# Squares for the key and query norms: one ScalarE instruction per PSUM bank, summed on VectorE

## The chip, the cores and the metric

The kernel runs on one core of a Trainium2 chip. The metric is the device time of one execution in microseconds; a time given for a kernel is the median of its runs.

## The reference

A decoder layer of three blocks, each followed by a residual add and a LayerNorm, for 4 batches of 256 tokens of width 512. The first block is a small attention inside each token; the third is a top-8 mixture of 64 bias vectors. The second, where nearly all the work is, is a cross attention with 32 query heads in 8 groups of 4, over 1601 context rows and the 256 tokens themselves. Its queries and keys are normalized over their 128 numbers per head before the scores are formed:

```python
def rms_norm(x, w):
    var = jnp.mean(jnp.square(x.astype(jnp.float32)), axis=-1, keepdims=True)
    return (x.astype(jnp.float32) * jax.lax.rsqrt(var + EPS)).astype(x.dtype) * w

kv = jnp.concatenate([context, latents], axis=1)
q = (latents @ Wq).reshape(bsz, q_len, HEADS, HEAD_DIM).transpose(0, 2, 1, 3)
k = (kv @ Wk).reshape(bsz, kv_len, KV_HEADS, HEAD_DIM).transpose(0, 2, 1, 3)
v = (kv @ Wv).reshape(bsz, kv_len, KV_HEADS, HEAD_DIM).transpose(0, 2, 1, 3)
q = rms_norm(q, q_norm_w)
k = rms_norm(k, k_norm_w)
scores = jnp.einsum('bhgqd,bhkd->bhgqk', qg, k) * scale
probs = jax.nn.softmax(scores.astype(jnp.float32), axis=-1).astype(q.dtype)
out = jnp.einsum('bhgqk,bhkd->bhgqd', probs, v)
...
return out @ Wo
```

## The kernel before

**Units and heads.** The cross attention is cut into 32 units: 4 batches times 8 key/value heads, batch by batch. A unit has 4 query heads. Products are made as three fp16 matmuls of high and low parts (`mm3`, lines 241 to 243), so fp32 accuracy comes from fp16 operands.

**The work of a unit on keys and values.** The 1857 rows of a batch are 15 tiles of 128 rows (the last one of 65), taken as 7 pairs and one single. `kv_proj` projects a pair into one PSUM bank `kvp` (for each tile 128 columns of keys and 128 of values). ScalarE then squares the keys of each tile with `accum_out`, which gives the sum over the 128 columns in `kss` (L403). GpSimd scales the sums and takes them to the power of -1/2 (L405, L406: `krk`). ScalarE writes the high part of the values `Vh` (L411) and VectorE the low part `Vl` (L412). `kv_n` is emitted later: ScalarE writes the normalized keys' high part `kh` (L426), VectorE the low part (L428), which also releases the bank. A DMA transposes `kh` into `KT`.

**The work of a unit on queries.** `q_proj` projects each of the 2 tiles of 128 tokens into one bank `qp` (4 heads of 128 columns). ScalarE squares each head with `accum_out` into `qss` (L449), GpSimd makes `qrq` (L451, L452), VectorE the normalized queries `qn` (L459), and `q_tr` splits and transposes them. The tile `qn` has one buffer: it receives the squares first, and the normalized queries then overwrite them.

**The work of a head.** `qk` makes the scores of a pair of key tiles in a bank `s`; ScalarE copies it to SBUF (L498) and VectorE takes a running maximum (L502, L504, L507), after which the bank is free. `qmax`, `qmax_t` and `qmax_b` find and spread the maximum (L514 to L536). `soft` subtracts it on VectorE (L545), makes the exponentials on ScalarE (L553, L554) and the low part on GpSimd (L555); in batch 0 one of four chunks is done with one exponential and a GpSimd copy (L550, L551). `pv` multiplies with the values (L574 to L576), `oevac` divides (L584 to L593), `wout` applies the output weights.

**Order.** Every step is put on a list with a position, in units of heads, from tables of offsets (`AT`, `F0` for batch 0, `LAST` for the last 4 units), and the list is emitted in order of position; the start has an order written out by hand (`START`), in which two units and the first block's attention share the engines. The framework's scheduler then orders the instructions on each engine from its own timeline model (`schedule_with_timeline_sim=True`), so a change of one instruction can move others. Each engine runs its instructions in the order that results.

**PSUM.** Six banks with the tag `u` serve `kvp`, `qp`, `s`, the output products and transposes alike; one bank each serves the maxima and the sums of `pv`.

Of the kernel before, what the change touches and what calls it, by code (L numbers as in the profile page):

```python
# [12 lines left out]
AF = mybir.ActivationFunctionType  # L13
ALU = mybir.AluOpType
AX = mybir.AxisListType
# [3 lines left out]
P = 128  # L19
# [32 lines left out]
def tile_decoder(ctx: ExitStack, tc: tile.TileContext, x, cx, Wq1, bq1, Wk1, bk1, Wv1, bv1,  # L52
                 Wq, Wk, Wv, Wo, qnw, knw, rw, rb, eb, out):
    nc = tc.nc
# [7 lines left out]
    G = Wq.shape[1] // Wk.shape[1]  # L62
# [174 lines left out]
    def mm3(dst, quads, start=True, stop=True, skip=False):  # L237

        n = len(quads)
        for k, (ah, al, bh, bl) in enumerate(quads):  # L240
            nc.tensor.matmul(dst, ah, bh, start=start and k == 0, stop=False, skip_group_check=skip)  # L241
            nc.tensor.matmul(dst, ah, bl, start=False, stop=False, skip_group_check=skip)  # L242
            nc.tensor.matmul(dst, al, bh, start=False, stop=stop and k == n - 1, skip_group_check=skip)  # L243
# [64 lines left out]
    def nk(t):  # L308
        return REM if t == NT - 1 else P

    def kview(tile_, t):

        o = (t % 2) * 2 * NC * P
        return tile_[:, o:o + 2 * NC * P].rearrange("p (l c k) -> p l c k", l=2, c=NC)[:, :, :, :nk(t)]

    def tiles_of(p):
        return [t for t in (2 * p, 2 * p + 1) if t < NT]
# [57 lines left out]
    KT, VT, QT = {}, {}, {}  # L375
    kns, qns = {}, {}
    PW = XS * WS

    kring = [const.tile([P, NT, 2, P], F16, name=f"KT_{i}") for i in range(2)]
    VR = 19  # L380
# [9 lines left out]
    def kv_proj(u, p):  # L390
        h, b = units[u]
        wkv = Wt["kv", h]
        ts_ = tiles_of(p)
        n = len(ts_)
        k = nk(ts_[0])
        ps = psu.tile([P, 2, 2 * P], F32, tag="u", name=f"kvp_{u}_{p}")
        for j, t in enumerate(ts_):
            v = kview(kvt[u, p], t)
            mm3(ps[:k, j, :], [(v[:, 0, c], v[:, 1, c], wkv[:, 0, c], wkv[:, 1, c]) for c in range(NC)])
        ss = p2.tile([P, 2], F32, tag="kss", name=f"kss_{u}_{p}")  # L400
        kn = p2.tile([P, 2, P], F32, tag="kn", name=f"kn_{u}_{p}", bufs=2)
        for j in range(n):
            nc.scalar.activation(kn[:k, j, :], ps[:k, j, 0:P], AF.Square, accum_out=ss[:k, j:j + 1])  # L403
        rk = p2.tile([P, 2], F32, tag="krk", name=f"krk_{u}_{p}")
        nc.gpsimd.tensor_scalar(ss[:k, :n], ss[:k, :n], 1.0 / (P * QS * QS), 1e-6 * PW * PW / (QS * QS), ALU.mult, ALU.add)  # L405
        nc.gpsimd.tensor_tensor(rk[:k, :n], ss[:k, :n], mhalf[:k, :n], ALU.pow)  # L406
        v = NPAIR * u + sum(q[0] == u for q in vuse.values())
        assert v < VR or ("pv", *vuse[v - VR]) in done
        vuse[v] = (u, p)
        vh, vl = VT[u, p] = vring[v % VR]  # L410
        nc.scalar.activation(vh[:k, :n, 0:P], ps[:k, :n, P:], AF.Copy, scale=VS / PW)  # L411
        nc.vector.scalar_tensor_tensor(vl[:k, :n, :], ps[:k, :n, P:], VS / PW, vh[:k, :n, 0:P],  # L412
                                       ALU.mult, ALU.subtract)
        kns[u, p] = (kn, rk, ps)
# [25 lines left out]
    def q_proj(u, i):  # L440
        h, b = units[u]
        wq = Wt["q", h]
        ps = psu.tile([P, G, P], F32, tag="u", name=f"qp_{u}_{i}")
        v = kview(kvt[u, TL], NF + i)
        mm3(ps.rearrange("p g d -> p (g d)"), [(v[:, 0, c], v[:, 1, c], wq[:, 0, c], wq[:, 1, c]) for c in range(NC)])
        ss = p2.tile([P, G], F32, tag="qss", name=f"qss_{u}_{i}")
        qn = p2.tile([P, G, P], F32, tag="qn", name=f"qn_{u}_{i}", bufs=1)
        for g in range(G):
            nc.scalar.activation(qn[:, g, :], ps[:, g, :], AF.Square, accum_out=ss[:, g:g + 1])  # L449
        rq = p2.tile([P, G], F32, tag="qrq", name=f"qrq_{u}_{i}")  # L450
        nc.gpsimd.tensor_scalar(ss, ss, 1.0 / P, 1e-6 * PW * PW, ALU.mult, ALU.add)  # L451
        nc.gpsimd.tensor_tensor(rq, ss, mhalf[:, :G], ALU.pow)  # L452
        qns[u, i] = (qn, rq, ps)
# [237 lines left out]
    for i in range(NQ):  # L691
        first[f"a{i}"] = lambda i=i: next(x0[i], None)
        first[f"lwq{2 * i}"] = lambda i=i: wload_q(0, 2 * i)
        first[f"wq{2 * i}"] = lambda i=i: wprep_q(0, 2 * i)
        for k, f in (("qproj", q_proj), ("qnorm", q_n), ("qturn", q_tr)):
            first[f"{k}{i}"] = lambda f=f, i=i: f(0, i)
# [4 lines left out]
    for p in range(NPAIR):  # L701
        for k, f in (("load", src_load), ("make", kv_make), ("keep", lambda b, p: kv_keep(b, p, kvt[b, p]))):
            first[f"{k}{p}"] = lambda f=f, p=p: f(0, p)
        for k, f in (("proj", kv_proj), ("norm", kv_n), ("turn", kv_tr)):
            first[f"{k}{p}"] = lambda f=f, p=p: [f(u, p) for u in range(HB)]
# [54 lines left out]
    for u in range(U):  # L760
        h, b = units[u]
        A = par(u)
        if u > 0:
            t0 = 4 * (u - 1)
            if u > 1:
                at(t0 - 0.01, proj_new, u)
            steps = [("kv", p) for p in range(NPAIR) if p != TL]
            z = A["z0"] if h == 0 else A["z1"]
            steps[z:z] = [("kv", TL), ("q", 0), ("q", 1)]
            if u == 1:  # L770
                steps = [("q", 0), ("q", 1)] + 8 * [("", 0)]
            step = A["span"] / len(steps)
            for k, (what, v) in enumerate(steps):
                pos = t0 + step * k
                norm, turn = min(pos + A["norm"] * step, 4 * u - 0.006), min(pos + A["turn"] * step, 4 * u - 0.005)
                if what == "kv" and u > 1:
                    at(pos - A["lead"] * step, kv_load, u, v)
                    at(pos, kv_proj, u, v)
                    at(norm, kv_n, u, v)
                    at(turn, kv_tr, u, v)  # L780
                elif what == "q":
                    at(pos, q_proj, u, v)
                    at(norm, q_n, u, v)
                    at(turn, q_tr, u, v)
        z = "l" if u == U - 1 else ""
        for g in range(G):
            n = 4 * u + g
# [55 lines left out]
```

## Time and profile before

| | before |
|---|---|
| median of 3 runs | 2420.73 us (2419.91 to 2424.31) |
| profiled execution | 2421.83 us, span 2420.1 us |
| granted TensorE clock, mean | 0.991 |
| DMA | 338.82 MB, mean 140 GB/s |
| squares of keys with sums (L403), ScalarE | 480 squares, 480 read-outs of the sum |
| squares of queries with sums (L449), ScalarE | 256 squares, 256 read-outs of the sum |

The page lists busy time by engine, then by line: the line and engine, the operation, what it writes and reads, the count, the busy time, the mean of one in ns, and the idle time just before, with what ended it. Matmuls overlap in TensorE's pipeline, so the mean of one is longer than the time from one start to the next. ScalarE's and VectorE's rows overlap a little too.

### The profile page before, as it was taken

How to read it: one execution, taken by the hardware profiler on the slowest of the kernel's cores; microseconds unless marked ns; L12 is line 12 of the kernel's file. 1: busy time of each engine (PE TensorE's matmuls, PEld its weight loads, DVE VectorE, ACT ScalarE, POOL GpSimd, SP SyncE). 2: the span in 40 equal slices, each digit the busy share in tenths (PEclk: the TensorE clock that was granted, in tenths of full speed). 3: DMA queues.
4: the chain of work that ended last, by engine and by line, in shares of the span. 5: the costliest groups of instructions: out<-in, count | busy, mean ns of one | idle time of the engine just before them, and what ended most of it. 6: DMA issues, size and time to landing. Idle time of an engine off the chain costs nothing.

```text
span 2420.1 us, 65667 instructions
## 1 busy us (share of the span) xinstructions
PE 2347.3 (97%) x25424; PEld 2003.1 (83%) x25424; DVE 1909.9 (79%) x3747; ACT 2051.1 (85%) x4672; POOL 1538.5 (64%) x1367
## 2 busy tenths in 40 slices
PE   7799999999999999999999999999999999999997
PEld 5587888888888878888888888888888888888885
DVE  8788978987877788787777788787777778777775
ACT  4798898888888878889888888888889888889884
POOL 2377776776666655776656666666666655657554
PEclk9999999999999999999999999999999999999997
DMA  8946776666564546555545555455644543554310
GB/s 267 245 100 160 185 175 178 185 153 156 137 164 112 148 139 166 139 142 125 151 128 129 156 142 137 140 138 121 156 116 113 131 122 109 140 131 105 98 35 27
DMA packets 393345, 338.82 MB, mean 140 GB/s; under 512 B 318532, under 2 KB 328260, under 8 KB 384840
## 3 DMA queue, kind: packets, MB, share of 16 engines
q1 hardware_dynamic: 393032, 334.63, 53.0%
q8 instruction: 199, 3.26, 0.6%
q14 instruction: 114, 0.93, 0.2%
HBM read 219.98 MB, written 38.80 MB: 107 GB/s over the span
## 4 chain that ended last, share of the span: by engine, by line
PE 74%; ACT 8%; DVE 7%; issue 5%; POOL 4%; DMA 2%; SPq 0%; POOLq 0%; DVEq 0%; ACTq 0%
PE o L574 7%; PE o L576 7%; PE o L575 7%; PE kvp L241 7%; PE kvp L243 7%; PE s L241 7%; PE kvp L242 7%; PE s L243 7%; PE s L242 7%; PE wo L241 2%; PE wo L242 2%; PE wo L243 2%; POOL P L555 2%; DVE S L545 2%; ACT P L553 2%
## 5 line engine op out<-in xcount | busy, mean ns | idle before, releaser
L555 POOL TENSOR_TENSOR P<-S,P 128x1024 f16<-128x1024 f32 (+1 forms) x512 | 1032.3, 2027 | 435.3 <-ACT S L554 410.3
L574 PE MATMUL o<-Vh,P 128*128 128x129 f16 (+1 forms) x3840 | 696.1, 221 | 6.8 <-ACT P L553 2.9
L576 PE MATMUL o<-Vh,P 128*128 128x129 f16 (+1 forms) x3840 | 695.8, 220 | 3.6 <-POOL P L555 3.6
L575 PE MATMUL o<-Vl,P 128*128 128x128 f16 (+1 forms) x3840 | 695.0, 219 | 0.0
L498 ACT COPY S<-s 128x512 f32<-128x512 f32 (+1 forms) x1024 | 568.3, 594 | 81.8 <-PE s L243 75.4
L553 ACT ACTIVATE P<-S,lnps 128x1024 f16<-128x1024 f32 (+1 forms) x480 | 530.9, 1117 | 48.1 <-DVE S L545 46.8
L545 DVE TENSOR_TENSOR S<-S,mt 128x1024 f32<-128x1024 f32 (+1 forms) x512 | 557.8, 1146 | 13.1 <-PE mt L536 12.2
L554 ACT ACTIVATE S<-S,lnps 128x1024 f32<-128x1024 f32 (+1 forms) x480 | 538.4, 1126 | 0.2
L241 PE MATMUL s<-QT,KT 128*128 128x256 f16 x1920 | 524.0, 273 | 14.1 <-ACT S L498 3.1
L243 PE MATMUL s<-QT,KT 128*128 128x256 f16 x1920 | 523.9, 273 | 0.0
L242 PE MATMUL s<-QT,KT 128*128 128x256 f16 x1920 | 523.7, 273 | 0.0
L504 DVE TENSOR_TENSOR M<-s,M 128x512 f32<-128x512 f32 x640 | 438.5, 685 | 99.8 <-ACT S L498 79.6
L574 PEld LDWEIGHTS <-P 128*128 128x128 f16 (+1 forms) x3840 | 376.1, 98 | 24.6 <-DVE oh L593 3.3
L241 PE MATMUL kvp<-wkv_back,kv 128*128 128x256 f16 (+1 forms) x1440 | 392.6, 273 | 1.8 <-DVE rl L584 0.6
L243 PE MATMUL kvp<-wkv_back,kv 128*128 128x256 f16 (+1 forms) x1440 | 392.6, 273 | 0.0
L242 PE MATMUL kvp<-wkv_back,kv 128*128 128x256 f16 (+1 forms) x1440 | 392.6, 273 | 0.0
L575 PEld LDWEIGHTS <-P 128*128 128x128 f16 (+1 forms) x3840 | 377.4, 98 | 14.7
L576 PEld LDWEIGHTS <-P 128*128 128x128 f16 (+1 forms) x3840 | 375.6, 98 | 5.0 <-POOL P L555 3.8
L241 PEld LDWEIGHTS <-kv 128*128 128x128 f16 (+1 forms) x2040 | 201.5, 99 | 48.0 <-issue 8.0
L243 PEld LDWEIGHTS <-kv 128*128 128x128 f16 (+1 forms) x2040 | 201.4, 99 | 47.1
L242 PEld LDWEIGHTS <-kv 128*128 128x128 f16 (+1 forms) x2040 | 201.4, 99 | 41.4 <-issue 1.7
L241 PEld LDWEIGHTS <-KT 128*128 128x128 f16 x1920 | 188.0, 98 | 33.1 <-issue 5.5
(177 smaller groups left out, 4164.2 us busy)
## 6 DMA issues: line engine op xcount, KB each, us to landing
kv<-kvd SPq DMA_DIRECT2D x210, 512.0 KB, 3.7
wq_back<-wqd SPq DMA_DIRECT2D x24, 1024.0 KB, 6.2
wo_back<-wod SPq DMA_DIRECT2D x24, 1024.0 KB, 5.2
kvd<-kvm SPq DMA_DIRECT2D x28, 512.0 KB, 3.1
cst<-in_ctx_dram SPq DMA_DIRECT2D x24, 512.0 KB, 5.8
wkv_back<-wkvd SPq DMA_DIRECT2D x24, 512.0 KB, 4.2
st_q<-in_L_xattn_Wq_dram SPq DMA_DIRECT2D x17, 512.0 KB, 4.8
wqd<-wq SPq DMA_DIRECT2D x8, 1024.0 KB, 6.1
```

What stands on the lines that cost most here:

```text
L241: nc.tensor.matmul(dst, ah, bh, start=start and k == 0, stop=False, skip_group_check=skip)
L242: nc.tensor.matmul(dst, ah, bl, start=False, stop=False, skip_group_check=skip)
L243: nc.tensor.matmul(dst, al, bh, start=False, stop=stop and k == n - 1, skip_group_check=skip)
L498: nc.scalar.copy(sv, ps[:, :m, :])
L504: nc.vector.tensor_tensor(Mx[n], ps, Mx[n], ALU.max)
L545: nc.vector.tensor_tensor(sv, sv, Mb[n].unsqueeze(1).broadcast_to([P, m, S]), ALU.subtract)
L553: nc.scalar.activation(pt[:, 0, :m, :], sv, AF.Exp, bias=lnps, scale=ES)
L554: nc.scalar.activation(sv, sv, AF.Exp, bias=lnps, scale=ES)
L555: nc.gpsimd.tensor_tensor(pt[:, 1, :m, :], sv, pt[:, 0, :m, :], ALU.subtract)
L574: nc.tensor.matmul(a[:, :P + 1], ph, v1[:k], start=t == 0 and i == 0, stop=False, skip_group_check=True)
L575: nc.tensor.matmul(a[:, :P], ph, v0[:k], start=False, stop=False, skip_group_check=True)
L576: nc.tensor.matmul(a[:, :P + 1], pl, v1[:k], start=False, stop=t == NT - 1 and i == NQ - 1, skip_group_check=True)
```

## The change

The squares of a bank are made by one ScalarE instruction without a sum: two tiles of keys together (256 columns), and the four heads of a query tile together (512 columns). VectorE then adds them up over the innermost 128 columns. The switch `SQE` selects VectorE for the sum (1) or GpSimd; it is 1. GpSimd's steps, and everything behind them, stay as they are. The lines of the kernel below the first added line move down by one.

```diff
@@ -375,6 +375,7 @@
     PW = XS * WS
+    SQE = 1
@@ -399,8 +400,8 @@ def kv_proj
         ss = p2.tile([P, 2], F32, tag="kss", name=f"kss_{u}_{p}")
         kn = p2.tile([P, 2, P], F32, tag="kn", name=f"kn_{u}_{p}", bufs=2)
-        for j in range(n):
-            nc.scalar.activation(kn[:k, j, :], ps[:k, j, 0:P], AF.Square, accum_out=ss[:k, j:j + 1])
+        nc.scalar.activation(kn[:k, :n, :], ps[:k, :n, 0:P], AF.Square)
+        (nc.vector if SQE else nc.gpsimd).tensor_reduce(ss[:k, :n], kn[:k, :n, :], AX.X, ALU.add)
@@ -445,8 +446,8 @@ def q_proj
         ss = p2.tile([P, G], F32, tag="qss", name=f"qss_{u}_{i}")
         qn = p2.tile([P, G, P], F32, tag="qn", name=f"qn_{u}_{i}", bufs=1)
-        for g in range(G):
-            nc.scalar.activation(qn[:, g, :], ps[:, g, :], AF.Square, accum_out=ss[:, g:g + 1])
+        nc.scalar.activation(qn, ps, AF.Square)
+        (nc.vector if SQE else nc.gpsimd).tensor_reduce(ss, qn, AX.X, ALU.add)
```

## The prediction

> **What bounds the kernel now.** I read the page first. Its first part gives the busy time of each engine, and the stretch sums cut the span into start, batch 0, the long middle and the end (columns: span of the stretch, then busy time and count of PE, PEld, DVE, ACT, POOL, the granted clock, DMA share, GB/s).
>
> ```profile
> PE 2347.3 (97%) x25424; PEld 2003.1 (83%) x25424; DVE 1909.9 (79%) x3747; ACT 2051.1 (85%) x4672; POOL 1538.5 (64%) x1367
> ```
>
> ```profile
> 0.00:120.00 120.00, 86.58 (x667) 68.24 (x668) 95.70 (x175) 73.72 (x212) 38.50 (x82) 0.95 0.90 258
> 120.00:580.00 460.00, 451.29 (x4981) 389.09 (x4980) 387.48 (x721) 401.83 (x905) 338.66 (x283) 0.99 0.65 162
> 580.00:2340.00 1760.00, 1748.29 (x19170) 1498.72 (x19169) 1374.83 (x2745) 1529.70 (x3491) 1125.00 (x983) 1.00 0.50 132
> 2340.00:2420.00 80.00, 61.16 (x615) 47.02 (x612) 51.91 (x108) 45.88 (x66) 36.37 (x22) 0.84 0.07 23
> ```
>
> TensorE is the bound. It stands still for 72.8 us in all (2420.1 - 2347.3): 33.4 in the first 120 us, 8.7 up to 580, 11.7 in the next 1760, 18.8 at the end. The change takes no work from TensorE, so what it can win lies in these 72.8 us alone, and the 20.4 us between 120 and 2340 are the part that ScalarE and VectorE, as feeders, can touch. What it can lose has no such bound. Next, the waits of PE alone show whom the feeders make late.
>
> ```profile
> PE kvp L241 <- DVE M L504: 5.7, 6, 1.9
> PE s L241 <- ACT S L498: 3.1, 5, 0.9
> PE o L576 <- POOL P L555: 3.6, 1, 3.6
> ```
>
> VectorE is named more often than ScalarE. Summed over the rows of that view between 120 and 580 us, PE waits 7.7 us for VectorE and 0.8 for ScalarE; between 580 and 2340, 7.5 and 3.8. So the engine that gets work is the one that already holds TensorE up, and the engine that is relieved hardly does.
>
> **The change, ScalarE's side.** 32 units of work each make 7 full pairs of key tiles, one part pair of 65 rows and 2 query tiles. The timeline of ScalarE gives the pace (start of a row to start of the next).
>
> ```profile
> 1199.48 0.57 ACT L498 COPY S<-s 128x512 f32<-128x512 f32 x1
> 1199.95 1.15 ACT L553 ACTIVATE P<-S,lnps 128x1024 f16<-128x1024 f32 x1
> ...
> 1201.25 0.29 ACT L449 ACTIVATE qn<-qp 128x128 f32<-128x128 f32 x1
> ...
> 1202.26 1.18 ACT L554 ACTIVATE S<-S,lnps 128x1024 f32<-128x1024 f32 x1
> ...
> 1204.12 0.30 ACT L403 ACTIVATE kn<-kvp 128x128 f32<-128x128 f32 x1
> 1204.28 0.24 ACT L403 ACTIVATION_READ_ACCUMULATOR kn<-kvp 128x1 f32 x1
> ...
> 1204.62 0.43 ACT L411 ACTIVATE Vh<-kvp 128x256 f16<-128x256 f32 x1
> 1204.89 0.64 ACT L498 COPY S<-s 128x512 f32<-128x512 f32 x1
> ```
>
> Each square with a sum is two instructions, the second one reading out the sum. Four of them for a query tile hold ScalarE for 1.01 us (1201.25 to 1202.26), two for a key pair for 0.50 (1204.12 to 1204.62). One instruction on 256 columns of a bank paces at 0.27 (L411), on 512 at 0.47 (L498); one on 128 at 0.16, its read-out not counted. Saved: 224 x 0.23 = 51.5, 64 x 0.54 = 34.6, 32 x 0.09 = 2.9, together 89 us, 2.8 per unit of some 72 us. The Trainium skill, page "ScalarE: Activation LUTs", section "What ACT_TABLE_LOAD costs", prices an ACTIVATE with immediate operands at 186 ns + 0.833 ns per column, 93 ns of it overlapped, and has no price for the read-out. By it the saving would be an estimated 39 us (224 x 0.09 + 64 x 0.28), less than half; the relief below would shrink with it, and the total would come out 0.6 us higher.
>
> **VectorE's side.** It gets 320 reduces. For 128x256 the nearest row is L214, also a reduce of 256 numbers a row: 0.33 us on the chain. For 128x512 it is L514, with L504, an elementwise operation of the same size, as the control.
>
> ```profile
> L504 DVE TENSOR_TENSOR M<-s,M 128x512 f32<-128x512 f32 x640 | 438.5, 685 | 99.8 <-ACT S L498 79.6 <-DVE M L504 0.5
> L514 DVE TENSOR_REDUCE M<-M 128x256 bf16<-128x512 f32 x128 | 89.2, 697 | 3.8
> ```
>
> 697 ns alone, and 0.60 when packed (a 512-column step of L502 on the chain). 224 x 0.33 = 73.9, 64 x 0.60 = 38.4, 32 x 0.20 = 6.4 (between the 163 ns of a two-element reciprocal, L584, and 0.33): 119 us, 3.7 per unit; by full durations (697, and 418 as the 256-column Vl step L412 takes) some 143. A rule speaks against the move: the Trainium skill, "VectorE: DVE Perf Modes", section "Rules for kernel authors", calls `tensor_reduce` the slowest operation of the engine. The rows do not bear that out at this size, 697 against 685, so I charge no extra; a reduce twice as slow as elementwise work would make it about 240 us.
>
> What of this is covered? In the built order nearly every reduce stands just ahead of the Vl of its own pair (L412 before). The waits show VectorE idle there: DVE Vl L412 <- ACT Vh L411, 78.4 us in 82 waits, about 1 us each. The square now ends 0.5 us sooner than Vh did, so in those 82 of 256 the reduce (0.33) lies in idle time and costs nothing. For the others it pushes what is queued behind it: Vl, then the L504 maxima that free PSUM banks, and the subtractions L545 before the exponentials. POOL's two small steps (L405, L406) now wait for the reduce, and the L555 behind them too; but POOL has 36% idle, and PE waits for L555 once, 3.6 us, so I price this at nothing, with up to 1 us per unit if VectorE is late.
>
> **The start.** From 20 to 56 us the chain runs almost only on VectorE, because both units' pairs and the small attention share it.
>
> ```profile
> 31.10 0.33 DVE big L214
> ...
> 70.33 1.15 ACT qn L449 x8
> ```
>
> Eight reduces stand in VectorE's order before the row that ends this stretch: 8 x 0.33 = +2.6 us. ScalarE's saving there is not on that path. The query squares on the chain, 1.15 us, become 0.47 + about 0.6 + a hand-over: no change.
>
> **The sum.** From 120 to 580 us VectorE gets 6.4 units x 3.7 = 24 us; its free share falls from 15.8% to 10.5%. If PE's wait on it goes as the inverse, 7.7 becomes 11.6: +3.9. From 580 to 2340, 92 us: free share 21.9% to 16.7%, 7.5 becomes 9.8: +2.3. A third of it is covered as above: 6.2 x 0.68 = 4.2. ScalarE's free share rises by about 4 points everywhere; the 4.6 us waited on it fall by a quarter: -1.1. Sum: 2.6 + 4.2 - 1.1 = +5.7 us. The profiled execution took 2421.83 (span 2420.1), 1.1 above the median of 2420.73 and within the spread of the three runs, so the forecast is 2420.73 + 5.7 = 2426.4, say 2426.5. 0.2%, about what a measurement of this kernel can tell from no change, is 4.8 us.
>
> **Rivals.** *ScalarE's relief counts after all (faster).* Half of the 20.4 us of mid idle goes because S copies (L498) and exponentials come sooner, and the start's reduces fit the gaps marked "issue" on the chain: 10.2 less 2 lost on VectorE, 2412 to 2413. For it: ScalarE is the fuller feeder (85%), and VectorE waits 79.6 us on the copies of L498. Against it: PE itself hardly waits for ScalarE. It decides if VectorE's idle time covers over two thirds of the reduces rather than one.
> *All covered (no change).* VectorE has 510 us idle and takes 119; if the start's 2.6 are hidden too, only the scheduler's reshuffle is left, about 2421.
> *VectorE clogs batch 0 (clearly slower).* At 89% to 92% a burst of four L545 (1.13 us each) with a reduce ahead of it delays maxima and so PSUM banks: a further 1.5 us in each of 6.4 units, and half of that later, 24 x 0.3: about 2440. For it: VectorE's slices at 90% and PE's waits on L504 lie in this stage. It decides from about 93% of VectorE between 240 and 480 us.
> *It does not do what it says.* The built order has 320 squares instead of 736, and 320 reduces on VectorE, none on POOL, so I give this no chance.
>
> **How the numbers follow.** Mildly slower, as summed (2425.6 to 2433): 0.30. Clogged: 0.14. No change (2415.9 to 2425.6): 0.29. Faster: 0.27. The instructions are ordered anew on every engine: of the 320 small POOL steps, 75 stand before or behind another L555 than they did. That moves small idle times in either direction and keeps the other cases near. The range leaves about one in ten at each end: 2412 (the relief case) to 2443 (clogged, with 3 us more at the start).
>
> **What would show it.** Right: no read-out rows on L403/L449's successors, ScalarE down by 60 to 90 us, VectorE up by 110 to 145, PE idle in the first 120 us up from 33.4 to about 36, PE's waits on VectorE rows up by 3 to 5, on ScalarE rows down. Wrong: PE's mid idle falls below 15 us (relief wins), reduces well over 0.45 us, POOL's L555 among PE's waits, or a lower granted clock.

## The result, and the profile after

The changed kernel takes 2463.05 us, the median of 4 runs (2457.03 to 2465.57), against 2420.93 (2419.91 to 2424.31) before: a ratio of 1.0166, 95% interval 1.0154 to 1.0178, or 42 us more. The profiled execution took 2461.62 us, with a span of 2459.8 and a mean granted clock of 0.988 (0.991 before). Forecast were 2426.5 and a range up to 2443. The sign was right; the size was 6 us instead of 42.

Busy time by engine, from the page of the kernel after:

```profile
PE 2357.5 (96%) x25424; PEld 2006.5 (82%) x25424; DVE 2024.8 (82%) x4067; ACT 1972.8 (80%) x3520; POOL 1533.7 (62%) x1367
```

ScalarE lost 78 us and VectorE gained 115, as forecast (-89 and +119). TensorE stands still for 102.3 us (2459.8 - 2357.5) instead of 72.8. These 29.5 us and 10.2 us of longer busy time, at a granted clock that is 0.3% lower (0.3% of 2347 is 7 us), make up the span's 39.7.

The stretch sums of the kernel after (columns as before):

```profile
0.00:120.00 120.00, 88.56 (x646) 67.73 (x646) 94.39 (x184) 58.70 (x128) 31.07 (x78) 0.93 0.82 236
120.00:580.00 460.00, 428.56 (x4671) 365.80 (x4670) 399.64 (x746) 373.53 (x653) 324.79 (x268) 0.99 0.60 158
580.00:2340.00 1760.00, 1741.14 (x19076) 1494.13 (x19073) 1449.42 (x2972) 1462.34 (x2621) 1119.24 (x985) 1.00 0.50 133
2340.00:2460.00 120.00, 99.19 (x1041) 78.86 (x1038) 81.34 (x168) 78.24 (x122) 58.58 (x38) 0.90 0.11 31
```

Read the count behind TensorE's busy time as well as the time. In the first 120 us TensorE is busy for longer than before, at a lower clock, but has made 21 matmuls fewer; between 120 and 580 it makes 310 fewer and stands still for 31.4 us instead of 8.7. To follow this without the stretches' fixed edges, I matched the two traces by the last running maximum of each unit (L514 before, L515 after). The kernel after lags by 12.2 us at the end of unit 0, by 14.6 at unit 3, 21.3 at unit 4, 32.7 at unit 7, and by only 7 more at the end. So the start and batch 0 lose 33 us, and the other three batches 7.

From the waits of PE alone, kernel after, the rows on the maxima and the one on L556 (line waited for; us in all, times, longest):

```profile
PE kvp L241 <- DVE M L505: 7.7, 7, 1.5
PE wo L241 <- DVE M L505: 7.0, 2, 4.7
PE s L241 <- DVE M L505: 6.3, 12, 1.3
...
PE o L577 <- POOL P L556: 4.1, 2, 3.9
```

Before, the second of these rows was

```profile
PE wo L241 <- DVE M L504: 1.6, 1, 1.6
```

Most of it is a wait that was there before, only longer: a matmul wants a PSUM bank whose last reader is a maximum on VectorE (17.1 of the 26.2 us that PE waits for VectorE between 120 and 580 us). Summed as in the prediction, PE's waits on VectorE grow from 7.7 to 26.2 us between 120 and 580 us, and from 7.5 to 17.0 between 580 and 2340; its waits on ScalarE in the second of these stretches fall from 3.8 to 1.3, but in the first 120 us they grow from 2.7 to 7.3.

The reduce itself costs what was forecast (groups of VectorE by shape, kernel after: count, busy us, mean ns, then idle time before it and its releaser):

```profile
L404 DVE TENSOR_REDUCE kss<-kn 128x2 f32<-128x256 f32 x224 | 92.5, 413 | 55.1 <-ACT kn L403 54.6
L450 DVE TENSOR_REDUCE qss<-qn 128x4 f32<-128x512 f32 x64 | 43.7, 682 | 30.9 <-ACT qn L449 30.6
```

New is what stands behind it. GpSimd's own waits, first before, then after:

```profile
POOL kss L405 <- ACT Vh L411: 82.6, 21, 7.1
POOL kss L405 <- ACT kn L403: 63.6, 48, 14.7
POOL qss L451 <- ACT qn L449: 47.9, 33, 3.9
```

```profile
POOL kss L406 <- DVE kss L404: 233.5, 73, 17.3
POOL qss L452 <- DVE qss L450: 79.6, 33, 7.6
```

From 194 us to 313: GpSimd stands in its order in front of the two small steps of the norm and waits for the reduce, which has its own place in VectorE's queue. Matched row by row, the time from the end of the square to the finished norm grows from 3.20 to 5.05 us on average, and a bank `kvp` is held from its last matmul to its last read (L428, L429 after) for 10.68 instead of 9.22 us. The longest single stop of PE in batch 0 shows how such queues meet (timelines of GpSimd, VectorE, ScalarE and PE, kernel after):

```profile
447.46 7.89 POOL L556 TENSOR_TENSOR P<-S,P 128x1024 f16<-128x1024 f32 x4
450.07 5.58 DVE L215 TENSOR_TENSOR sc<-sc,mx 128x256 f32<-128x256 f32 x1
451.09 0.41 ACT L403 ACTIVATE kn<-kvp 128x256 f32<-128x256 f32 x1
455.56 0.68 DVE L505 TENSOR_TENSOR M<-s,M 128x512 f32<-128x512 f32 x1
456.30 0.61 PE L241 MATMUL wo<-wo,OT 128*128 128x512 f16 x1 [4.66 <-DVE M L505]
457.35 0.41 DVE L404 TENSOR_REDUCE kss<-kn 128x2 f32<-128x256 f32 x1
457.92 0.19 POOL L406 TENSOR_SCALAR kss<-kss 128x2 f32<-128x2 f32 x1 [2.20 <-DVE kss L404]
```

A small subtraction on VectorE (L215, median 0.43 us) lasts 5.58, until 0.3 us after GpSimd's four L556. The maximum behind it is late, and TensorE stands 4.66 us for its bank. The square made at 451.09 has its sum only at 457.76, and GpSimd has by then waited 2.20 us for it; before the change that sum would have been read out on ScalarE at once. What begins this stop, though, is the drawn-out subtraction (the last section shows why) and not the longer chain: the sum is late because of it. In the kernel before, three of the six such subtractions were drawn out too (1.05 to 1.95 us).

### The profile page after: what moved, and what is told of

Same layout as the page of the kernel before. It is cut to its first block, busy times and chain, and to the rows that moved or that the text cites. A ratio compares the mean times of both kernels' runs of the same rounds, so it can differ in the third digit from the quotient of the medians.

```text
span 2459.8 us, 64727 instructions
## 1 busy us (share of the span) xinstructions
PE 2357.5 (96%) x25424; PEld 2006.5 (82%) x25424; DVE 2024.8 (82%) x4067; ACT 1972.8 (80%) x3520; POOL 1533.7 (62%) x1367
## 5 line engine op out<-in xcount | busy, mean ns | idle before, releaser
L556 POOL TENSOR_TENSOR P<-S,P 128x1024 f16<-128x1024 f32 (+1 forms) x512 | 1031.2, 2025 | 340.3 <-ACT S L555 297.4
L499 ACT COPY S<-s 128x512 f32<-128x512 f32 (+1 forms) x1024 | 558.2, 579 | 97.9 <-PE s L243 90.9
L555 ACT ACTIVATE S<-S,lnps 128x1024 f32<-128x1024 f32 (+1 forms) x480 | 531.1, 1110 | 0.3
L505 DVE TENSOR_TENSOR M<-s,M 128x512 f32<-128x512 f32 x640 | 439.0, 686 | 92.7 <-ACT S L499 74.8
L427 ACT ACTIVATE kh<-kvp,krk 128x128 f16<-128x128 f32 (+1 forms) x480 | 156.3, 384 | 103.5 <-POOL krk L407 90.5
```

What stands on the lines that cost most here:

```text
L499: nc.scalar.copy(sv, ps[:, :m, :])
L505: nc.vector.tensor_tensor(Mx[n], ps, Mx[n], ALU.max)
L555: nc.scalar.activation(sv, sv, AF.Exp, bias=lnps, scale=ES)
L556: nc.gpsimd.tensor_tensor(pt[:, 1, :m, :], sv, pt[:, 0, :m, :], ALU.subtract)
```

## The experiments

Three theories. **Work**: VectorE has 115 us more to do, so its maxima come late. **Chain**: the way from the square to the norm is longer by a hand-over through a second in-order queue, so GpSimd and the banks of `kvp` come free later, whatever the work. **Order**: the scheduler lays out the instructions anew, and any other order than the one before is worse. Costs in us are against the median of the kernel before in the same set of runs (2421.8 to 2423.8). All of them hold the kernel before unless "change" is said.

**The work alone.** The sums stay on ScalarE and are used; VectorE makes 320 reduces as well, into a tile that nobody reads.

```diff
+        sx = p2.tile([P, 2], F32, tag="kssx", ...)
+        nc.vector.tensor_reduce(sx[:k, :n], kn[:k, :n, :], AX.X, ALU.add)   # and the same for qn
```

> The sums stay on ScalarE as before; VectorE makes all 320 reduces as in the change, into a tile that nobody reads. Work theory (VectorE's 120 us fall into stages where it has little to spare): +30 to +50 us over before, with PE's lag growing in the start and in heads 16 to 28 as in the change. Chain theory (what costs is that the sums pass through VectorE's queue, so that GpSimd, ScalarE and the PSUM bank behind them wait): within 8 us of before. Order theory (any new instruction makes the scheduler lay out a worse order): +10 to +40 us, not tied to the amount of work.

2441.93 us, ratio 1.0076 [1.0061, 1.0091]: +18. The bank of `kvp` is held for 9.61 us. VectorE's work by itself costs less than half of what the change does, and in the same place: matched as above, this kernel lags by 19.4 us at the end of unit 7 and by 20.1 at the end.

**The chain alone, by a copy.** ScalarE sums as before, but VectorE hands the sums on.

```diff
-            nc.scalar.activation(kn[:k, j, :], ps[:k, j, 0:P], AF.Square, accum_out=ss[:k, j:j + 1])
+            nc.scalar.activation(kn[:k, j, :], ps[:k, j, 0:P], AF.Square, accum_out=sx[:k, j:j + 1])
+        nc.vector.tensor_copy(ss[:k, :n], sx[:k, :n])                       # and the same for qss
```

> Squares and sums stay on ScalarE; VectorE only copies the 2 or 4 sums of a bank to the tile that GpSimd reads, some 0.1 us each. Work theory: +5 to +10 us (some 25 to 30 us of VectorE time, a quarter of the change's). Chain theory: +25 to +45 us, GpSimd's wait in front of its first step on the sums as long as in the change (some 230 us for keys). Order theory: +10 to +40 us.

2478.15 us, 1.0223 [1.0208, 1.0239]: +54, more than the change and than any theory expected. But the copy was not cheap (group of VectorE, this kernel):

```profile
L405 DVE COPY kss<-kssx 128x2 f32<-128x2 f32 x224 | 166.9, 745 | 64.4 <-ACT kn L404 63.2
```

Two numbers a row for 745 ns: chain and a stall on VectorE are mixed here, so the hop was made twice more.

**The chain alone, by a reduce over one element, and by ScalarE.**

```diff
+        nc.vector.tensor_reduce(ss[:k, :n], sx[:k, :n].unsqueeze(2), AX.X, ALU.add)   # the first
+        nc.scalar.copy(ss[:k, :n], sx[:k, :n])                                        # the second
```

> As the earlier run in which VectorE only hands the sums on, but by a reduce over one element instead of a copy. In that run the copy of 2 numbers took 745 ns on average and ended 22 to 27 ns after GpSimd's instruction whenever one was under way, so it had added 167 us of VectorE time and was no test of the chain alone. Chain theory: still +20 to +40 us, with the reduces at some 0.1 to 0.15 us each. Work theory (the copies' stall was the cost): within 8 us of before.

> ScalarE itself copies the sums to the tile that GpSimd reads: one more hand-over in the chain, no VectorE. Chain theory by its length alone: +10 to +30 us. Chain theory by VectorE's queue: within 6 us of before. Order theory: +5 to +15 us, as in the run with one square and no sum.

2469.73 us, 1.0192 [1.0177, 1.0207], +47, by VectorE; 2467.45, 1.0185 [1.0168, 1.0202], +45, by ScalarE. Both are above what any theory expected (up to +40 and +30). The hop itself is cheap in both (groups by shape, first the one by VectorE, then the one by ScalarE):

```profile
L405 DVE TENSOR_REDUCE kss<-kssx 128x2 f32<-128x2 f32 x224 | 33.1, 148 | 73.2 <-ACT kn L404 72.0
```

```profile
L405 ACT COPY kss<-kssx 128x2 f32<-128x2 f32 x224 | 58.5, 263 | 0.3 <-POOL krk L408 0.3
```

Neither has the change's work on VectorE (some 47 us in the one, none in the other) nor its relief of ScalarE, yet each loses as much in all as the whole change. So one more link can cost this, whichever engine makes it. But it costs it in another place. At the end of unit 7 the hop by VectorE lags by 23.1 us and the one by ScalarE by 12.0; up to the end they lose a further 26.4 and 31.2. The change loses 32.7 and then 6.7, with the same link in every unit. That the totals agree therefore does not show that the hop makes the change's loss.

GpSimd's waits do not settle it either. In the hop by VectorE they are much those of the change, in the one by ScalarE they are not (first the one by VectorE, then two rows of the one by ScalarE):

```profile
POOL kss L407 <- DVE kss L405: 256.5, 82, 16.9
```

```profile
POOL kss L407 <- ACT kss L405: 116.9, 65, 15.5
POOL qss L455 <- ACT qss L453: 64.1, 39, 5.3
```

These two are 181 us, less than the 194 of the kernel before; a further 75.3 us stand in front of the low part of the exponentials (L559 here), put down to the same copy.

The copy's 134 us more of VectorE time (166.9 against 33.1, keys alone) cost only some 7 us on top of the hop, less than the 18 of the work alone.

**The relief alone.** One square per bank, no sums at all: the norm is made from a constant, so the outputs are not normalized by the data.

```diff
-        for j in range(n):
-            nc.scalar.activation(kn[:k, j, :], ps[:k, j, 0:P], AF.Square, accum_out=ss[:k, j:j + 1])
+        nc.scalar.activation(kn[:k, :n, :], ps[:k, :n, 0:P], AF.Square)
...
-        nc.gpsimd.tensor_scalar(ss[:k, :n], ss[:k, :n], 1.0 / (P * QS * QS), ...
+        nc.gpsimd.tensor_scalar(ss[:k, :n], kn[:k, :n, 0], 0.0, 0.2 * PW * PW / (QS * QS), ...
```

> One square per bank on ScalarE without a sum and no reduce at all: GpSimd takes a constant in place of the mean square, but still waits for the squares, so the norms are left out of the computation. Work and chain theories: -6 to +3 us of before, since TensorE hardly waits for ScalarE. Order theory: +10 to +40 us, as in any other new mix of instructions.

2436.16 us, 1.0049 [1.0034, 1.0064]: +12, though ScalarE has 82 us less to do, no engine has an instruction more, and the bank is held as long as before (9.23 us). Relief of ScalarE by itself gains nothing, and something that only takes work away costs 12 us, all of it up to the end of unit 7 (12.9 us of lag there and at the end). Of the three theories only order speaks to that.

**By part and by place.** The change for the keys only, for the queries only; in the first 8 units (batch 0) only, in the others only.

```diff
+        if u < KVH:     # first 8 units; the other kernel has u >= KVH
...                      # square and reduce as changed
+        else:           # squares with accum_out as before
```

> The change on the keys alone, the queries as before. Work theory: two thirds of the VectorE time, +25 to +30 us. Chain theory: 256 of the 320 hand-overs, +30 to +36 us. Order theory: no tie to the share, anything from +5 to +40 us.

> The change on the queries alone, the keys as before. If the parts add up, the rest of the change's 42 us over the keys' 30: +12 us. Work theory: 39 of 119 us of VectorE time, +10 to +14. Chain theory: 64 of 320 hand-overs, +6 to +9 us. Order theory: anything to +15.

> The change in the start and batch 0 alone (8 of 32 units). By the places of the lag, and if the parts add up with the run of batches 1 to 3 alone (+9): +30 to +36 us. A reshuffle that has nothing to do with the place would not add up.

> The change in batches 1 to 3 alone (24 of 32 units); the start and batch 0 as before. All theories that put the loss where VectorE is fullest: a quarter of the loss or less, +5 to +12 us, since the change's lag grows by 32.7 us up to the end of batch 0 and by 7 after it. A loss tied to the number of hand-overs: three quarters, +30 us.

Keys 2453.38, 1.0126 [1.0109, 1.0143], +30; queries 2436.44, 1.0054 [1.0039, 1.0069], +14. Batch 0 2451.93, 1.0120 [1.0103, 1.0137], +30; the rest 2431.50, 1.0037 [1.0025, 1.0049], +9. Both pairs add up to about the change's 42 (44 and 39), and some 70% lies in a quarter of the units. The kernel with batch 0 changed lags by 11.7 us after unit 0, 35.8 after unit 7 and 32.6 at the end. A longer hold does not set the price by itself: with the change the banks of full pairs are held for 11.74 instead of 9.93 us in batch 0 and for 10.41 instead of 9.30 in the others, and the losses are 33 and 7.

**Is any new order worse?** Offsets of the list are moved: `norm`, the place of the normalization, by 0.02 of a head, and, in another kernel, by 0.22 everywhere, so that banks would be held longer.

```diff
-          ..., norm=1.091, ...
+          ..., norm=1.111, ...      # nudge_a; hold_alone has 1.311, and +0.22 in F0 and LAST too
```

> The kernel before, with one offset of the emission list moved by 0.02 of a step (norm 1.091 to 1.111): no work, no wait is added, only the scheduler's order changes a little. Order theory: +5 to +20 us, the price of any new order. Chain and work theories: within 5 us of before.

> The kernel before, with the normalization of keys and queries emitted 0.22 of a step later (norm 1.091 to 1.311, in batch 0 0.349 to 0.569, in the last units 1.251 to 1.471), some 1.5 us, so that the PSUM banks of projections are held about as much longer as in the change (9.2 to 10.7 us after the last matmul), without any new instruction or hand-over. Chain theory by way of the banks: +20 to +40 us. Chain theory by way of GpSimd's queue alone, and the work theory: within 8 us. Order theory: +5 to +20 us.

2422.99 us, 1.0002 [0.9993, 1.0012], and 2421.54, 0.9998 [0.9989, 1.0008]: nothing. The second did not do what it was meant to: the scheduler put the steps back, and the banks were held 9.30 us. What it does say is that the list can be moved without loss.

Then both kernels with the scheduler's timeline model off, so that each engine keeps the list's order.

```diff
-  schedule_with_timeline_sim=True
+  schedule_with_timeline_sim=False
```

> The kernel before without the scheduler: every engine takes its instructions in the order of the emission list. Slower than before, by some per cent or more; it is the reference for the next run.

> The change without the scheduler, so that its instructions stand in the same order as in the run without it, the squares joined and the reduces put in. Chain and work theories: 20 to 60 us slower than the kernel before without the scheduler. Order theory: within 10 us of it, or faster, since no order is laid out anew.

2796.12 us, 1.1537 [1.1520, 1.1554], without the change and 2808.08, 1.1587 [1.1570, 1.1605], with it, both against the kernel before: 12 us between them, which lies between what the order theory (up to 10) and the others (20 to 60) expected. In an order that isn't laid out anew the change costs 12, not 42; but that is another program, in which TensorE waits elsewhere, and the banks are not held longer with the change (7.74 against 8.06 us). It bounds nothing in the real one.

**Is it the banks?** A late last reader: after the low part of `kh`, GpSimd copies a column of it, and ScalarE reads one column of the bank once that is there.

```diff
+        nc.gpsimd.tensor_copy(dep[:k], kh[:k, 0, 1, 0:1])
+        nc.scalar.activation(dmy[:k], ps[:k, 0, 0:1], AF.Copy, scale=dep[:k, 0:1])
```

> The kernel before, and behind each pair's last normalization step one GpSimd copy of a column and one ScalarE read of one PSUM column that waits for it, into tiles that nobody uses: the bank of the projected keys is held some 1 to 2.5 us longer, while norms and keys are ready as early as before. Bank theory: +25 to +50 us. Theory of late norms: +3 to +12 us, for 256 more small instructions on GpSimd and ScalarE. Order theory: +10 to +20.

2487.58 us, 1.0273 [1.0258, 1.0288]: +65. From its first matmul to its last read a bank is now held for 15.41 us (12.19 before, 13.63 in the change). This agrees with a price on held banks, but does not show it: the added read also puts 79 us of rows (70.2 + 9.1) in ScalarE's queue, each behind one of 256 new copies on GpSimd.

The other way round, the keys are copied to SBUF at once, so that the norm no longer holds a bank, without and with the change.

```diff
+        nc.scalar.copy(kraw[:k, :n, :], ps[:k, :n, 0:P])     # squares and kh then read kraw, not ps
```

> The control: the kernel before with the same copy to SBUF. Bank theory: -8 to +8 us, as banks are freed earlier but TensorE already runs without a gap in most stretches and ScalarE gets 60 us more. Theory of late norms: +5 to +15 us, for a chain longer by the copy. If this run is below 2415 us, it is a version that beats both.

> The change, with the projected keys copied to SBUF by ScalarE as soon as they are there (0.27 us a pair, some 60 us in all); squares and normalization read the copy, so that the bank is free some 3 us after its last matmul whatever the norms do. Bank theory: most of the loss goes, within 12 us of the kernel before, although ScalarE works more. Theory of late norms: still +35 to +50 us. Order theory: +10 to +40.

2493.94 us, 1.0302 [1.0287, 1.0317], and 2533.24, 1.0458 [1.0442, 1.0473]. The bank came free earlier (held for 7.5 us from its first matmul to its last read, against 12.19), but the step behind it doubled (group of VectorE, kernel without the change):

```profile
L430 DVE SCALAR_TENSOR_TENSOR kh<-kraw,krk,kh 128x128 f16<-128x128 f32 x448 | 280.2, 657 | 16.9 <-ACT kh L428 15.8 <-DMA st_q<-in_L_xattn_Wq_dram 0.4
```

It took 342 ns with its input in PSUM (L428). VectorE had 157 us more to do, so the pair says nothing of the banks; that the change still cost 39 us here says that freeing `kvp` early does not by itself remove the loss.

Last, a seventh bank for the ring, taken from the maxima, which join it.

```diff
-    psu = ctx.enter_context(tc.tile_pool(name="psu", bufs=6, space=PSUM))
+    psu = ctx.enter_context(tc.tile_pool(name="psu", bufs=7, space=PSUM))
...
-        bank = psm.tile([P, 512], F32, tag="m", name=f"mt_{n}")
+        bank = psu.tile([P, 512], F32, tag="u", name=f"mt_{n}")
```

> The kernel before with the same ring of seven. Bank theory: TensorE waits 22.7 us for banks of the ring here, so up to 15 us faster, 2405 to 2420 us; the gap to the change with the same ring shrinks to 10 to 30 us. Order theory: 2425 to 2460 us, since the order is laid out anew, and the gap stays about 42 us.

> The change, with the PSUM bank of the maxima put into the ring of banks for projections and scores: seven banks for all of them instead of six and one. The maxima hold a bank for part of the time only, so the ring gains about half a bank; the change's longer hold takes 0.2 (4.09 banks held on average against 3.89). Bank theory: 15 to 40 us of the loss come back, 2425 to 2450 us. Theory of late norms, and order theory: 2455 to 2475 us, no gain.

2449.17 us, 1.0112 [1.0095, 1.0129], without the change and 2473.13, 1.0205 [1.0189, 1.0221], with it. The difference between the two shrinks from 42 to 24 us, and PE's waits for banks of the ring, worked out from the traces, fall from 22.7 to 8.0 us and from 42.4 to 15.0. The gap is what the bank theory expected (10 to 30), the times themselves are what the order theory did (2455 to 2475 with the change, 2425 to 2460 without it). A bank more made the kernel before slower by 27, with a wait that was 4.1 us there (waits of PE, without the change):

```profile
PE mt L523 <- DVE M L513: 40.3, 23, 8.6
```

Relieved in one place, the order made a new stop in another. None of these kernels beats the one before.

**Over the kernels with six banks** and the scheduler's model on, the copies to SBUF left aside, PE's waits for ring banks (PE's standstill before the first matmul into a bank, as far as the bank's last reader had not ended) go with the loss, if not strictly: 22.7 us before and with the nudge, 26.0 with `norm` moved by 0.22, 25.5 queries only, 26.1 relief, 28.2 later units only, 31.0 work, 39.6 batch 0 only, 40.3 keys only, 42.4 the change, 42.3 the hop by a copy, 46.7 and 46.5 the two cheap hops, 55.8 the late reader. For the change that is 19.7 us more, of the 29.5 that TensorE stands still longer: banks that come late are the larger part of that standstill, and half of the loss.

**What stays open.** Each by itself, against the kernel before, the hop costs 45 to 47 us, VectorE's work 18 and the relief 12. That is 75 or more where the change costs 42, so they are not parts that add up; work and relief lose where the change does, the hop mostly elsewhere. What the change's 42 us are made of is not shown. All of it acts through the order that the scheduler then lays out, and two kernels that only relax something (relief, +12; seven banks, +27) lose as well. No run held the real order fixed and added one ingredient alone. Nor was one more rival tested apart, VectorE's steps stalled behind GpSimd (last section): the time by which VectorE's steps exceed the tenth percentile of their group (those by over 60 ns) is 10.2 us in the first 600 us before and 16.8 after.

## Why the prediction was wrong

**Right.** TensorE is the bound, and VectorE the feeder that holds it up; what ScalarE saves (78 of 89 us) and VectorE gains (115 of 119); a reduce is no dearer than elementwise work (413 and 682 ns against 415 for the Vl step and 685), so the rule that speaks against it was rightly not charged; the sign; and, in the rival "VectorE clogs batch 0", the place: start and batch 0, on PE's waits for the L504 maxima (L505 after). That rival's sum is not what its words say: half of 1.5 us is 0.75, not 0.3, and with 24 x 0.75 it gives about 2454, outside the range and nearer to the 2463 measured.

**Wrong, first and most: "I price this at nothing, with up to 1 us per unit if VectorE is late".** This is the step that put GpSimd's L405 and L406 behind the reduce. The argument was GpSimd's 36% idle time and its one wait with PE behind it. Idle time of an engine was no cover for a link on a chain: GpSimd's waits grew from 194 to 313 us, the way from square to norm by 1.85 us and the hold of a `kvp` bank by 1.5 us on average. One hop by itself measured 45 to 47 us; even the bound of 1 us per unit, 32 us, was too low, and it stood in the text as a bound but not in the sum nor in the range. How much of the change's 42 us it makes stays open: in batches 1 to 3, where the hop alone loses 26 to 31 us, the change loses 7. L555 among PE's waits, named as a sign of being wrong, moved only from 3.6 to 4.1 us.

**Wrong: VectorE's work, 2.6 + 4.2 = +6.8.** The reduces alone, with no hop and no relief, measured 18, so this term was too small whatever the hop does.

**Wrong in it: the law of the free share.** VectorE's share between 120 and 580 us went from 84% to 87%, and PE's waits on it from 7.7 to 26.2 us, not to 11.6; later from 7.5 to 17.0, not to 9.8. The clog rival was to decide "from about 93% of VectorE between 240 and 480 us". That condition was not met, while its outcome was exceeded (stretch sums, first the kernel after, then the hop by a one-element reduce; VectorE is the third number in turn behind PE and PEld):

```profile
240.00:480.00 240.00, 223.31 (x2393) 187.55 (x2391) 210.47 (x390) 190.41 (x339) 164.74 (x140) 0.99 0.67 171
```

```profile
240.00:480.00 240.00, 227.54 (x2446) 191.45 (x2445) 203.51 (x400) 199.99 (x460) 162.51 (x139) 0.99 0.70 171
```

210.5 of 240 us is 88%, and in the hop kernel VectorE is at 85% in a stretch where the kernel before has 86% (207.5), with TensorE 6.9 us short of the kernel before all the same. In the work alone VectorE is at 88% too (211.9 us), with TensorE 8.7 us short. How full VectorE is does not by itself tell the waits.

**Wrong: the start, +2.6.** Only the eight reduces were counted; the lag after unit 0 is 12.2 us, and 11.7 with the change in batch 0 only. No single ingredient gives this: it is 7.4 with the hop by VectorE, 2.5 with the hop by ScalarE, 6.7 with the relief and 1.7 with the work. TensorE's standstill in the first 120 us, forecast to rise from 33.4 to about 36, is 31.4, with fewer matmuls made.

**Wrong: the relief, -1.1.** PE's waits on ScalarE did fall, by 2.5 us in the middle, but the kernel with the relief alone lost 12. The prediction let "the scheduler's reshuffle" move small idle times in either direction; no laying out anew in these runs won anything.

**Wrong: the clock.** It fell from 0.991 to 0.988, which the prediction named as a sign of being wrong; TensorE's busy time rose by 10.2 us with it, as in the two cheap hops (2357.8 and 2362.7).

## What to carry to other kernels

When TensorE is at 97% and lives on a small ring of PSUM banks, the busy time that a change moves does not tell its price: 82 us off a feeder won nothing here, and a hand-over of 0.15 us through one more in-order queue cost 47 us. Treat every wait that a change adds in front of another engine's in-order queue as a term of the sum, with its end in the range. Before moving work between engines, try the hop alone, the work alone and the relief alone, and compare with the change not only the totals but also where in the span the loss arises: here the hop matched the total and not the place.

## What the runs showed of the hardware

**A copy of two numbers on VectorE waits for GpSimd.** The copies of 128x2 last from 158 ns (tenth percentile) to 2667. Of the 224, 146 began while a GpSimd instruction was under way, and these end 22 to 27 ns after it (tenth to ninetieth percentile); the other 78 take 145 to 170 ns. The reduce over one element in the same place takes 148 ns on average, stalled by nothing.

**A step with two inputs in SBUF does the same.** L430 takes 657 ns instead of 342 when one input moves from PSUM to SBUF; L215 took 5.58 us under four L556; and of the two-input splits of L92 (128x1024, `nat`) in the kernel before, the nine that began while a GpSimd instruction was under way took 1686 ns on average, the nine others 1220. The reduces of the change (L404, 128x256) took 414 and 411 ns in the two cases. The Trainium skill, page "SBUF — State Buffer", section "Who interferes with whom", has both: VectorE and GpSimd share a pair of ports that one of them holds for a whole instruction, copies and steps with two SBUF inputs may need it, and `tensor_reduce` never does. The rows here agree on all three points.
